# Experts' work between attention scores: smaller pieces, at least one in every round

## The chip, the cores and the metric

The kernel runs on one core of one Trainium2 chip. Its engines work side by side, each through its own queue in order: TensorE (PE; its weight loads are PEld in the profile), VectorE (DVE), ScalarE (ACT), GpSimd (POOL) and SyncE (SP, which here issues DMAs). They wait for each other through semaphores. The metric is the device time of one execution in microseconds, as the median of several runs. A profile is one further execution, taken by the hardware profiler; its span goes from the first to the last instruction.

## The reference

A block adds three things for 2048 tokens of 512 values: the input x, differential causal attention of the layer-normed x, and a mixture of experts of the layer-normed x. Cut to what matters here:

```
xn = layernorm(x)
# attention: 32 maps of 16 values, in pairs; 16 heads; causal
q, k = rotary(xn @ Wq), rotary(xn @ Wk);  v = xn @ Wv
a1 = softmax(mask(q1 @ k1.T * scale)) @ [v1, v2]
a2 = softmax(mask(q2 @ k2.T * scale)) @ [v1, v2]
f  = rfft(a1, tokens) - lambda * rfft(a2, tokens)
attn = irfft(f * gauss, tokens);  rms norm per head;  @ Wout
# experts: 8, the two best of each token, and a shared one of double width
y = sum over the two of w_e * (silu(xn @ w1[e]) * (xn @ w3[e])) @ w2[e]
shared = (silu(xn @ sw1) * (xn @ sw3)) @ sw2
out = x + attn + y + shared
```

## The kernel before

The kernel has a first part (layer norm, v, routing, rotated q and k, the shared expert for four of the 16 token tiles), the stage `middle`, and `ending` (the rest of the filter as products, the norm, the output projection, the sum). The change lies in `middle`. Of its two variants the one for scores of bounded size runs here, `middle(False)`. All five engines are under a manual schedule in it: each engine's instructions stand in the order in which the program issues them.

Attention goes through 32 chunks: for each of eight groups of two heads (`g`), four blocks of 512 queries (`qc`), the last block first. A chunk is a list of units. A unit is one tile of scores against 128 keys, for one head and both of its maps: two products on TensorE (L761) into one of two PSUM tiles, and one exponential on ScalarE (L774) into `pt`. Units on the diagonal, called masked, are narrower and are cut by GpSimd afterwards (L779). Chunks have 29, 21, 13 and 5 units, 544 in all. When both heads of a key block are there, their product with the values follows on TensorE (`values`, L801, into `ps_o`). VectorE adds the exponentials up (`added`, L818, or a copy L815 for the first). One round after a chunk's last values come its sums over keys (`sums`, L827) and, later in the same round, its `finish`: transposes of the output and of the sums (L839, L840), a reciprocal on VectorE (L842) and the normalised output `o_n` (L847). In the next round `put` (L856) adds the two halves into `vd` on GpSimd. When a group's four chunks are there, GpSimd does the first half of a Fourier transform over the 16 token tiles, in place (`folded`, L861 on, in seven steps). The last group's is on VectorE.

The main loop takes four units in each of 136 rounds. A round of the program before issues, in this order: a burst of two units; the values that the round before made ready, of one chunk; the sums of a closing chunk; a burst of the other two units; the remaining values; puts; additions; the `finish` of a closed chunk; experts' work until a budget is met, with the additions of the second two units between and behind its pieces; the additions of masked units; and up to two steps of folding.

Experts' work comes from a generator, `experts`. It yields after each piece the estimated time of that piece, and the loop asks for pieces as long as the time worked is behind the round's share of `work_all`. Its first 55 pieces are the shared expert's: `wh` (L231) and two halves of `wy` (L269) for each tile. The remaining ones are for 36 routed blocks of 128 tokens each. For block j these are:

- `up_first`: the product `xh` (L168), tanh on ScalarE (L175), a product on VectorE (L176)
- `up_third`: the product `xg` (L168), a product on VectorE (L182) that gives u; then the gather of the rows of block j + 2 on GpSimd (L585) and the fetch of up weights on SyncE
- `down` of block j - 1: the product `xy` (L201), scaled by ScalarE (L210) and stored; the fetch of down weights
- `turned_back` of block j: transposes of u on TensorE (L191) and two copies on VectorE (L193, L194)
- `transposed` of block j + 1: transposes of x on TensorE (L159) and a copy on ScalarE (L161)

The last three form one piece in the program before, after `xg`. All these tiles (`wh`, `wy`, `xh`, `xg`, `xy`, `ps_u`, `ps_x`) and also `ps_sum`, `ps_ot` and `ps_st` come from one PSUM pool of three banks, `fps`; a new tile takes the bank that was released first.

Of the kernel before, what the change touches and what calls it, by code (L numbers as in the profile page):

```python
# [19 lines left out]
P = 128  # L20
# [3 lines left out]
NT = T // P  # L24
# [3 lines left out]
TQ = QC // P  # L28
# [8 lines left out]
SCH = 6  # L37
TOP = 2
EARLY = 4
# [3 lines left out]
NR = NS - 3  # L43
# [19 lines left out]
def block_kernel(  # L63
# [17 lines left out]
    ys = dram.tile([NS * P, E], F32, name="ys")  # L81
# [16 lines left out]
    wcol = cpool.tile([P, NR], F32, name="wcol")  # L98
# [179 lines left out]
    with ExitStack() as pools:  # L278
# [231 lines left out]
        late = None  # L510
# [47 lines left out]
    def middle(general):  # L558


        with ExitStack() as pools:
# [29 lines left out]
            def experts():  # L591

                hidden = ExitStack()
                sp = hidden.enter_context(tc.tile_pool(name="shared", bufs=2))
                _, _, _, _, (_, _, stored), _ = expert(sp, fps, mp, by_scalar=True)
                _, _, _, chunks, result = shared_expert(sp, fps)
                for t0 in range(EARLY, NT - 1, TQ):
                    t1 = min(t0 + TQ, NT - 1)  # L600
                    last = t1 == NT - 1
                    cols = slice(t0 * P, t1 * P)
                    for n, us in enumerate(chunks(xnT[:, :, cols], u_last)):
                        if last and n == 0:
                            who_sb = mp.tile([P, E], F32, tag="x", name="who_sb")
                            who_sb = who_sb[:NR, : 2 * P].rearrange("n (p o) -> n p o", o=2)
                            nc.sync.dma_start(who_sb, who[: NR * P, :].rearrange("(n p) o -> n p o", p=P))
                        elif last and n == 3:
                            ps = bank([P, 2, NR], "ps_w")
                            for i in range(2):  # L610
                                nc.tensor.transpose(ps[:, i, :], who_sb[:, :, i], ident[:NR, :NR])
                            nc.vector.tensor_copy(tok, ps[:, 0, :])
                            nc.vector.tensor_copy(wcol, ps[:, 1, :])
                        elif last and n == 5:


                            xr = [rows_of(0), rows_of(1)]
                            es = [routed(0)]
                            fetch_up(es[0], 0, nc.sync)
                        yield 3.45 * (t1 - t0) / TQ  # L620
                    if last:
                        es.append(routed(1))
                        fetch_up(es[1], 1, nc.sync)
                    for t in range(t0, t1):
                        y = result(us, t - t0, range(NF))
                        yield 2.6
                        stored(result(us, t - t0, range(NF, SCH), y), ysh[t], 0.5)
                        yield 2.6
                hidden.close()
                rp = pools.enter_context(tc.tile_pool(name="routed", bufs=2))  # L630
                up_first, up_third, _, turned_back, (down, _, _), transposed = expert(rp, fps, mp, by_scalar=True)
                for i in range(2):
                    fetch_down(es[i], i, nc.sync)
                xT = transposed(xr.pop(0))
                yield 0.5
                for j in range(NR):
                    half = up_first(w_sb[j % 2][0], xT)
                    yield 2.4
                    u = up_third(w_sb[j % 2][0], xT, half)
                    if j + 2 < NR:  # L640
                        xr.append(rows_of(j + 2))

                    es.append(routed(j + 2) if j + 2 < NR else wex[NX + j + 2 - NR : NX + j + 3 - NR])
                    fetch_up(es[j + 2], j % 2, nc.sync)
                    yield 2.4
                    if j > 0:
                        down(*late)
                        fetch_down(es[j + 1], (j + 1) % 2, nc.sync)
                    uT = turned_back(u)
                    late = [(w_sb[j % 2][1], uT)], ys[j * P : (j + 1) * P, :], wcol[:, j : j + 1]  # L650
                    if j + 1 < NR:
                        xT = transposed(xr.pop(0))
                    if j == 1:
                        shared.append(True)
                    yield 3.7
                down(*late)
                yield 2.8

# [72 lines left out]
            class Chunk:  # L731
# [58 lines left out]
                def values(self, kb):  # L790

                    if self.done == 0:
                        self.o = vps.tile([P, QC], F32, tag="o", name="ps_o")
                    self.done += 1
                    first, self.ended = self.done == 1, self.done == (self.qc + 1) * TQ
                    for h in range(2):
                        v0 = 64 * self.g + 32 * h
                        pt, off = self.probs[h, kb]
                        for s in range(2):
                            r = 64 * h + 32 * s  # L800
                            nc.tensor.matmul(  # L801
                                self.o[r : r + 32, off:], vd[:, kb, v0 : v0 + 32], pt[:, s, :],
                                start=first, stop=self.ended, skip_group_check=True,
                            )
                    if self.ended:
                        self.o_sb = ap.tile([P, QC], F32, tag="o_sb", name="o_sb")
                        nc.scalar.copy(self.o_sb, self.o)
# [109 lines left out]
            for n, turn in enumerate(turns):  # L917
                chunk = Chunk(*turn)
                stream += [(n, chunk, unit) for unit in chunk.units()]
            work_all = (NT - 1 - EARLY) * ((2 * SCH - 1) * 3.45 / TQ + 5.2) + NR * 8.5 - 7.0  # L920
            ex = experts()
            for c in range(NQC):
                load_keys(0, c)
# [5 lines left out]
            def burst(units):  # L929
                nonlocal begun  # L930
                found = []
                for n, chunk, unit in units:
                    if n > begun:
                        begun = n
                        if n + 1 < len(turns):
                            load_queries(*turns[n + 1])

                        if chunk.g + 1 < NG:
                            load_keys(chunk.g + 1, (chunk.qc + 1) % NQC)
                    found += chunk.scores(unit)  # L940
                return found

            def values():

                chunk = todo[0][0] if todo else None
                while todo and todo[0][0] is chunk:
                    chunk.values(todo.pop(0)[1])
                return [chunk] if chunk is not None and chunk.ended else []

            def masked(entry):  # L950
                _, c, unit = entry
# [10 lines left out]
            for i in range(0, len(stream), 4):  # L962
                units = stream[i : i + 4]
                found = burst(units[:2])
                ended = values()
                for c in closing:
                    c.sums()
                    summed += 1
                found += burst(units[2:])
                while todo:  # L970
                    ended += values()
                todo += found
                for c in closed:
                    c.put(nc.gpsimd)
                    if c.qc == 0:
                        ready.append(c.g)
                closed, closing = closing, ended
                held, before = [], held
                added(before)
                added(u for u in units[:2] if not masked(u))  # L980
                later = [u for u in units[2:] if not masked(u)]
                for c in closed:
                    c.finish()
                while worked / work_all < (i + 4) / len(stream):
                    took = next(ex, None)
                    if took is None:
                        break
                    worked += took
                    added(later[:1])
                    later = later[1:]  # L990
                added(later)
                added(u for u in units if masked(u))
                for _ in range(0 if any(map(masked, units)) or not shared else 1 if len(ready) < 2 else 2):
                    if folding is None and ready:
                        folding = folded(ready.pop(0), nc.gpsimd)
                    if folding is not None and next(folding, 0) == 0:
                        folding = None
# [1 line left out]
                c.put(nc.gpsimd)  # L999
            ended = []  # L1000
            while todo:
                ended += values()
            for some in (closing, ended):
                for c in some:
                    c.sums()
# [369 lines left out]
```

## Time and profile before

| what | value |
|---|---|
| median of 3 runs | 1381.73 us (1381.63 to 1382.18) |
| the profiled execution's own time | 1382.72 us |
| its span | 1380.8 us |
| `middle`, by the first and the last product of its main part | 254.8 to 1262.6 us |
| units' products on TensorE (L761), busy | 209.9 us, 1280 matmuls |
| values (L801), busy | 270.7 us, 2560 matmuls |
| routed experts, xh, xg and xy, busy | 94.5, 93.2 and 103.5 us |
| additions on VectorE (L818), busy | 623.4 us, 576 instructions |
| exponentials on ScalarE (L774), busy | 528.1 us, 544 instructions |
| masks on GpSimd (L779), busy | 174.9 us, 256 instructions |

The rows with "busy" count the time in which at least one such instruction ran. Time of an engine before an instruction in which it did nothing is its idle time, and the profile names what ended it, written "<-" and the engine, tile and line that released it. The granted clock of TensorE is 1.00 or 0.50 in a window; its mean over the span is 0.987.

### The profile page before, as it was taken

What the parts mean: (1) busy time and instruction counts of PE and PEld (TensorE: products, weight loads), DVE (VectorE), ACT (ScalarE), POOL (GpSimd) and SP (SyncE); (2) the same over time, 40 slices, a digit from 0 to 9 for tenths busy, and PEclk for the clock granted to TensorE, in tenths of its full rate; (3) what the DMA queues carried; (4) which work ended last, traced back from release to release, by engine and by line L of the source; (5) the groups of instructions that cost most, each with busy time, mean ns of one, the idle gap of its engine ahead of it and who ended that gap; (6) DMA issues with size and microseconds to landing.
All of it is one profiled execution on the core that took longest, in us unless ns stands there. A gap on an engine that the chain in (4) does not pass through costs nothing.

```text
span 1380.8 us, 20566 instructions
## 1 busy us (share of the span) xinstructions
PE 1331.9 (96%) x7472; PEld 620.8 (45%) x7472; DVE 1005.4 (73%) x1337; ACT 692.7 (50%) x853; POOL 598.3 (43%) x673
## 2 busy tenths in 40 slices
PE   7999999899999999998899999999999999999998
PEld 3444444333443344444445444544454454445543
DVE  7059881368777776868677888867698779877785
ACT  2311110365656565665566566666667666662321
POOL 0002222012301232136975755757467537632874
PEclk9999999999999999999999999999999999999999
DMA  9406672200210121255455655656656565448996
GB/s 376 167 16 192 189 213 64 87 19 16 78 46 31 47 73 63 81 158 159 149 178 171 200 185 175 179 176 191 200 161 202 190 202 188 170 164 277 179 223 149
DMA packets 74689, 206.58 MB, mean 150 GB/s; under 512 B 12028, under 2 KB 12192, under 8 KB 69200
## 3 DMA queue, kind: packets, MB, share of 16 engines
q1 hardware_dynamic: 61840, 177.62, 39.4%
q0 software_dynamic: 11216, 23.31, 8.1%
q10 hardware_dynamic: 1520, 4.23, 0.9%
q8 instruction: 62, 1.02, 0.3%
q14 instruction: 51, 0.42, 0.1%
HBM read 161.26 MB, written 43.85 MB: 149 GB/s over the span
## 4 chain that ended last, share of the span: by engine, by line
PE 67%; DVE 5%; POOL 3%; DMA 3%; issue 2%; SPq 2%; ACT 2%; ACTq 0%; DVEq 0%; POOLq 0%
PE ps_o L801 17%; PE ps_s L761 12%; PE wh L231 8%; PE xy L201 6%; PE xh L168 6%; PE xg L168 6%; PE wy L269 4%; SPq L669 2%; PE ps_sum L827 2%; DVE sum L818 2%; ACT pt L774 1%; PE po L1196 1%; PE ps_ot L839 1%; PE ps_x L159 1%; DMA kS<-parts_k 1%
## 5 line engine op out<-in xcount | busy, mean ns | idle before, releaser
L818 DVE TENSOR_TENSOR sum<-sum,pt 128x1024 f32<-128x1024 f32 (+2 forms) x576 | 623.4, 1131 | 24.2 <-ACT pt L774 10.7
L774 ACT ACTIVATE pt<-ps_s 128x1024 f32<-128x1024 f32 x544 | 528.1, 1027 | 173.5 <-PE ps_s L761 128.1
L779 POOL TENSOR_SCALAR_AFFINE_SELECT pt<-pt 128x256 f32<-128x256 f32 x256 | 174.9, 708 | 340.5 <-ACT pt L774 277.5
L801 PE MATMUL ps_o<-pt,vd 128*32 128x512 f32 (+3 forms) x2560 | 270.7, 542 | 4.0 <-POOL pt L779 3.9
L761 PE MATMUL ps_s<-qS,kS 64*128 64x512 f32 (+3 forms) x1280 | 209.9, 411 | 14.7 <-ACT pt L774 12.9
L761 PEld LDWEIGHTS ps_s<-qS,kS 64*128 64x128 f32 x1280 | 97.8, 186 | 169.2 <-ACT pt L774 90.2
L231 PE MATMUL wh<-xnT,wu 128*128 128x512 f32 (+1 forms) x352 | 151.4, 578 | 0.0
L801 PEld LDWEIGHTS ps_o<-pt,vd 128*32 128x32 f32 x2560 | 67.2, 110 | 134.5 <-issue 115.5
L473 POOL DMA_INDIRECT who<-pairs,slot x32 | 34.3, 1073 | 202.0 <-DVE pairs L470 100.9
L520 PE MATMUL ps_x<-xnT,wqk_sb 128*128 128x512 f32 x256 | 110.5, 593 | 0.0
L201 PE MATMUL xy<-wd,uT 128*128 128x512 f32 (+1 forms) x216 | 103.5, 616 | 4.0 <-DVE rcp L842 4.0
L231 PEld LDWEIGHTS wh<-xnT,wu 128*128 128x128 f32 x352 | 64.9, 192 | 72.4 <-issue 57.3
L856 POOL TENSOR_TENSOR vd<-o_n 128x128 f32<-128x128 f32 x60 | 37.9, 653 | 137.2 <-DVE o_n L847 129.8
L168 PE MATMUL xh<-wu,xT 128*128 128x352 f32 x288 | 94.5, 471 | 0.7 <-ACT xT L161 0.7
L168 PE MATMUL xg<-wu,xT 128*128 128x352 f32 x288 | 93.2, 466 | 0.0
L520 PEld LDWEIGHTS ps_x<-xnT,wqk_sb 128*128 128x128 f32 x256 | 48.4, 190 | 60.6 <-issue 60.6
L269 PE MATMUL wy<-wd,ws 128*128 128x512 f32 x160 | 73.6, 601 | 0.0
L168 PEld LDWEIGHTS xh<-wu,xT 128*128 128x128 f32 x288 | 52.2, 191 | 33.6 <-issue 7.8
L168 PEld LDWEIGHTS xg<-wu,xT 128*128 128x128 f32 x288 | 52.6, 190 | 32.1 <-issue 4.3
L210 ACT ACTIVATE y_sb<-xy,wcol 128x512 f32<-128x512 f32 x36 | 24.8, 688 | 83.6 <-PE xy L201 83.6
L1052 POOL DMA_INDIRECT res<-ys,slot x32 | 56.6, 1769 | 21.0 <-DMA res<-ysh 10.4
L537 ACT CAST hi<-turned 128x1024 fp32r<-128x1024 f32 x16 | 16.7, 1045 | 93.8 <-DVE turned L535 83.1
(239 smaller groups left out, 1405.3 us busy)
## 6 DMA issues: line engine op xcount, KB each, us to landing
wu<-in_wex_dram SPq DMA_DIRECT2D x40, 1408.0 KB
wd<-in_wex_dram SPq DMA_DIRECT2D x39, 768.0 KB
kS<-parts_k SPq DMA_DIRECT2D x128, 128.0 KB
qS<-parts_q SPq DMA_DIRECT2D x256, 64.0 KB
ys<-y_sb SPq DMA_DIRECT2D x36, 256.0 KB
parts_q<-hi SPq DMA_DIRECT2D x32, 256.0 KB
parts_k<-hi SPq DMA_DIRECT2D x16, 256.0 KB
parts_k<-turned SPq DMA_DIRECT2D x16, 256.0 KB
```

The costliest lines, as they stand in the source:

```text
L168: nc.tensor.matmul(dst, xT[:, c, :], w[:, o : o + FI], start=(c == 0), stop=(c == NE - 1))
L201: nc.tensor.matmul(y, uT[:m, ic, :], w[:m, ic * E : (ic + 1) * E], start=(n == 0 and ic == 0), stop=(n == len(pairs) - 1 and ic == NF - 1),)
L231: nc.tensor.matmul(dst, w_sb[o // WUP][0][:, o % WUP : o % WUP + P], x[:, c, :], start=(c == 0), stop=(c == NE - 1))
L269: nc.tensor.matmul(y, us[i][:, t * P : (t + 1) * P], w_sb[i // NF][1][:, i % NF * E : (i % NF + 1) * E], start=(i == 0), stop=(i == SCH - 1),)
L520: nc.tensor.matmul(ps[:, i, :], wqk_sb[st, qk][:, i, c, :], xnT[:, c, cols], start=(c == 0), stop=(c == NE - 1),)
L761: nc.tensor.matmul(to, k, queries[2 * g + h, qc][r, off : off + w], start=True, stop=not general)
L774: nc.scalar.activation(pt[:, :, used], ps[:, :, used], AF.Exp, scale=SCALE)
L779: nc.gpsimd.affine_select(out=part, in_=part, pattern=[[0, 2], [1, P]], compare_op=ALU.is_ge, fill=0.0, base=0, channel_multiplier=-1,)
L801: nc.tensor.matmul(self.o[r : r + 32, off:], vd[:, kb, v0 : v0 + 32], pt[:, s, :], start=first, stop=self.ended, skip_group_check=True,)
L818: nc.vector.tensor_add(to, to, pt)
L856: eng.tensor_add(vd[:, self.qc * TQ : (self.qc + 1) * TQ, v0 : v0 + 32], self.o_n[:, :, h, 0, :], self.o_n[:, :, h, 1, :],)
L1052: nc.gpsimd.indirect_dma_start(out=came[k], out_offset=None, in_=ys, in_offset=bass.IndirectOffsetOnAxis(ap=slot[:, step - 2, order[k] : o ...
```

## The change

Four things change, all in `middle`.

1. In `experts`, a routed block's three pieces are cut elsewhere. The transposes of u of block j - 1 now stand at the head of block j's first piece, before `xh`; those of x of block j + 1 stand at the head of the third piece, before `xy` of block j - 1. The estimates become 2.9, 2.4 and 3.2 where they were 2.4, 2.4 and 3.7, and the budget `work_all` is 7.0 larger.
2. The loop asks for at least one piece in every round, also where the budget is already met.
3. Where the first values of a round are those of fewer than two key blocks, and no chunk is closing, one more piece is issued between the two bursts.
4. Two steps of folding in a round are taken only where none of the next round's units is masked.

```diff
@@ experts @@
-                xT = transposed(xr.pop(0))
-                yield 0.5
+                xT, late = transposed(xr.pop(0)), None
+                yield 0.6
                 for j in range(NR):
+                    if j > 0:
+                        late = [(w_sb[(j - 1) % 2][1], turned_back(u))], ys[(j - 1) * P : j * P, :], wcol[:, j - 1 : j]
                     half = up_first(w_sb[j % 2][0], xT)
-                    yield 2.4
+                    yield 2.9 if late else 2.4
                     u = up_third(w_sb[j % 2][0], xT, half)
...
                     yield 2.4
-                    if j > 0:
+                    if j + 1 < NR:
+                        xT = transposed(xr.pop(0))
+                    if late:
                         down(*late)
                         fetch_down(es[j + 1], (j + 1) % 2, nc.sync)
-                    uT = turned_back(u)
-                    late = [(w_sb[j % 2][1], uT)], ys[j * P : (j + 1) * P, :], wcol[:, j : j + 1]
-                    if j + 1 < NR:
-                        xT = transposed(xr.pop(0))
                     if j == 1:
                         shared.append(True)
-                    yield 3.7
+                    if late:
+                        yield 3.2
+                late = [(w_sb[j % 2][1], turned_back(u))], ys[j * P :][:P], wcol[:, j : j + 1]
+                yield 0.5
                 down(*late)
                 yield 2.8
@@ the loop @@
-            work_all = (NT - 1 - EARLY) * ((2 * SCH - 1) * 3.45 / TQ + 5.2) + NR * 8.5 - 7.0
+            work_all = (NT - 1 - EARLY) * ((2 * SCH - 1) * 3.45 / TQ + 5.2) + NR * 8.5
...
+            def work():
+                nonlocal worked
+                worked += next(ex, work_all)
...
                 found = burst(units[:2])
-                ended = values()
+                n, ended = values()
                 for c in closing:
                     c.sums()
                     summed += 1
+                if n < 2 and not closing:
+
+                    work()
                 found += burst(units[2:])
...
-                while worked / work_all < (i + 4) / len(stream):
-                    took = next(ex, None)
-                    if took is None:
-                        break
-                    worked += took
+                while True:
+                    work()
                     added(later[:1])
                     later = later[1:]
+                    if worked / work_all >= (i + 4) / len(stream):
+                        break
                 added(later)
                 added(u for u in units if masked(u))
-                for _ in range(0 if any(map(masked, units)) or not shared else 1 if len(ready) < 2 else 2):
+                if any(map(masked, units)) or not shared:
+                    steps = 0
+                else:
+                    steps = 1 if len(ready) < 2 or any(map(masked, stream[i + 4 : i + 8])) else 2
+                for _ in range(steps):
                     if folding is None and ready:
```

`values` now also returns how many key blocks it took.

More of the change, by code (lines that the diff above doesn't have):

```diff
@@ L943, in values @@
             def values():
-                chunk = todo[0][0] if todo else None
+                chunk, n = todo[0][0] if todo else None, len(todo)
                 while todo and todo[0][0] is chunk:
                     chunk.values(todo.pop(0)[1])
-                return [chunk] if chunk is not None and chunk.ended else []
+                return n - len(todo), [chunk] if chunk is not None and chunk.ended else []
+            def work():
+                nonlocal worked
+                worked += next(ex, work_all)
             def masked(entry):
@@ L968, in middle @@
                     summed += 1
+                if n < 2 and not closing:
+                    work()
                 found += burst(units[2:])
                 while todo:
-                    ended += values()
+                    ended += values()[1]
                 todo += found
@@ L1001, in middle @@
             while todo:
-                ended += values()
+                ended += values()[1]
             for some in (closing, ended):
```

## The prediction

> **What bounds the kernel now.** I read the page first, then the waits of TensorE between 255 and 1262 us (the stage that the change touches), its timeline around the longest of them, and the granted clock window by window.
>
> ```profile
> PE 1331.9 (96%) x7472; PEld 620.8 (45%) x7472; DVE 1005.4 (73%) x1337; ACT 692.7 (50%) x853; POOL 598.3 (43%) x673
> ...
> PE 67%; DVE 5%; POOL 3%; DMA 3%; issue 2%; SPq 2%; ACT 2%; ACTq 0%; DVEq 0%; POOLq 0%
> ```
>
> TensorE is busy for 96% of the span and carries the chain that ended last, and the change takes no matmul away. So a gain can only come from idle time of TensorE, and from its clock. In the stage, the idle time is this:
>
> ```profile
> PE ps_s L761 <- ACT pt L774: 12.9, 25, 2.2
> PE xy L201 <- DVE rcp L842: 4.0, 1, 4.0
> PE ps_o L801 <- POOL pt L779: 3.9, 2, 3.0
> PE ps_u L191 <- DVE rcp L842: 2.6, 1, 2.6
> PE ps_s L761 <- DVEq L1244: 1.7, 1, 1.7
> PE xh L168 <- ACT xT L161: 0.7, 1, 0.7
> PE ps_x L159 <- DVE o_n L847: 0.5, 1, 0.5
> PE ps_u L191 <- DVE xtanh L182: 0.3, 1, 0.3
> ```
>
> The columns are total us, times, longest. Together 26.6 us, half of them scores that wait for an exponential to free their PSUM tile. A wait costs more than its length, as the windows show (after the span: PE, PEld, DVE, ACT, POOL busy, then the clock):
>
> ```profile
> 901.30:904.70 3.40, 2.05 (x16) 0.76 (x20) 3.36 (x4) 2.91 (x4) 3.16 (x4) 0.99 0.12 39
> 904.70:908.10 3.40, 3.40 (x20) 0.89 (x12) 3.00 (x3) 0.86 (x1) 3.17 (x4) 0.50 0.80 185
> ...
> 976.30:979.80 3.50, 2.38 (x30) 1.03 (x30) 3.09 (x5) 3.40 (x4) 3.32 (x6) 1.00 0.94 344
> 979.80:983.20 3.40, 3.33 (x22) 1.53 (x19) 3.40 (x5) 2.43 (x3) 3.15 (x5) 1.00 0.47 110
> ```
>
> 1.35 us of idle in one window of 3.4 us is followed by a window at half clock, 1.1 us in another is not. A half window costs 1.7 us. The stage has eight: two at its start (256.1 to 262.9), two at 631.6, one each at 682.8, 775.0, 904.7 and 942.2.
>
> **The change, part by part.** I call a pass of the loop over four units a round and count from 0 to 135. Following both versions of the loop by hand gives the pieces in each round.
>
> *Waits for exponentials.* The 12.9 us are 2.23 in round 0, where nothing stands between the first two bursts; 0.34 in round 50; and the rest in the eight rounds with one pair of values between the bursts (8, 25, 42, 59, 76, 93, 110, 127; about 0.74 each, 1.71 in the one after the empty round 92) and behind the rounds without a piece (87, 97, 102: 1.34, 1.38, 0.66). The new loop puts a piece of at least 2.4 us into every one of these gaps, and two exponentials take 2 x 1.03 us. Only round 50 stays: -12.6. With them go the half windows at 904.7, 942.2 and the second at the start: -3 x 1.7 = -5.1.
>
> [...]
>
> *The order inside an expert's step.* Now u (three transposes, 0.33 us) stands ahead of the first product xh, and x (four, 0.44) ahead of the last, xy. A round or more lies between xg and u, and between x and xh: the waits of 0.7 (xT) and 0.3 (xtanh) go, -1.0.
>
> But three PSUM banks serve sums, ps_ot, ps_st and all experts' tiles. After a chunk's transposes (L839, L840) one bank is free; the next comes with the reciprocal L842, the third with o_n (L847), and both are behind the additions on VectorE:
>
> ```profile
> 760.88 0.27 PE L840 MATMUL ps_st<-cst,s_sb 128*128 128x128 f32 x1
> 760.99 2.53 PE L168 MATMUL xg<-wu,xT 128*128 128x352 f32 x8
> ...
> 768.13 2.74 PE L201 MATMUL xy<-wd,uT 128*128 128x512 f32 x6
> 773.43 0.55 PE L191 MATMUL ps_u<-cst,xtanh 128*128 128x128 f32 x3 [2.56 <-DVE rcp L842]
> ```
>
> ```profile
> 757.61 6.82 DVE L818 TENSOR_TENSOR sum<-sum,pt 128x768 f32<-128x768 f32 x6
> 764.34 1.29 DVE L815 COPY sum<-pt 128x1024 f32<-128x1024 f32 x2
> 765.55 0.26 DVE L842 RECIPROCAL rcp<-ps_st 128x16 f32<-128x16 f32 x1
> ```
>
> Round 68 needed one bank and did not wait, although the reciprocal came 4.65 us after ps_st; round 69 needed three and waited. Over all 32 chunks the reciprocal ends 0.30 us after ps_st in 16, 1.0 to 2.1 after in 13, and 6.33, 4.65 and 5.08 after in rounds 51, 68, 69. In the old order mostly one long product followed (cover 2.4 to 2.6 us). In the new one, 16 of the 21 turn-outs in the routed part begin with u or x, and the long product behind it needs the second bank after a cover of only 0.2 to 0.3 us. What I expect, lag minus cover, with the lag corrected for work moved before it:
> - 51: old lag 6.33, less 3.3 us more work in rounds 48 to 50: 2.9; 52: 0.5. 68: 4.65, less 1.6 (its round 67 has no tanh ahead of the additions, and 0.55 more work): 3.0; 69: 0.3.
> - 102: 1.5, 119: 0.7, 85: 0.2 (lags 1.36, 1.35, 2.13, moved by the rounds before); 48, where xh needs the third bank: 0.85.
> - 82, 94, 111, 128: VectorE takes its additions late behind a product of the same round, lags of 1.0 to 1.3: 3.3 together. The rest, at lag 0.3: 0.5 together.
>
> Sum 13.8, where the old waits (4.0 + 2.6 + 0.5) were 7.1: +6.7. Bounds: 5 if VectorE is on time in all but 51 and 68, so -2; 25 if it is late as below, so +18. I stay near the middle, because the lags of the trace are measured and only their shift is mine. These waits had three half windows (5.1), I expect two: -1.7.
>
> *Folding.* The step counts of all 136 rounds come out equal: wherever two steps ran, either no masked unit follows or only one head group was ready. This edit moves nothing. GpSimd still has an unbroken queue from 645 to 682 us and the masks of round 58 behind it; 0.6 us more work of TensorE before it: -0.6 of 3.9.
>
> *Switches.* In the chain a product behind scores takes 0.19 us longer than behind another product (xg 2.56 against 2.37, xy 2.77 against 2.58). Stretches of experts' work rise from 132 (four rounds had none) to 145 (one each, and nine between bursts): 13 x 0.19 = +2.5. If a switch from values costs nothing, +0.8.
>
> *The tail.* The old budget left xg, xy, u and xy to be done while the last two chunks close. From the end of the last scores (1245.4) to the first fold on VectorE (1261.6) took 16.3 us, all covered by TensorE. Now only u and xy (3.1) precede the values (2.3) and sums (0.9); additions end near 7.1 (8.2 before, with a tanh product and its wait ahead), then sums 1.0, copy 0.4, transposes 0.7, and 1.8 from reciprocal to fold: 11.0, so 5.2 less. But 2.56 + 2.56 + 2.77 = 7.9 us now lie before the last scores, and the last xy no longer hides beside the fold: +2.7. Bounds 0 and +6 (nothing of the closing shortened but 1.9).
>
> DMAs keep their number. The row gathers on GpSimd move with xg by a round or two, and land over 10 us before their use; the weight fetches on SyncE still have over 20 us to their product.
>
> **Sum**: -12.6 - 5.1 - 1.0 + 6.7 - 1.7 - 0.6 + 2.5 + 2.7 = -9.1 us on a span of 1380.8. The median of the runs is 1381.7 (the profiled execution 1382.7), so 1372.6.
>
> **Rivals.** (1) *The bank becomes the bound, slower.* If VectorE doesn't profit from the shifts in rounds 51 and 68/69 (6.1, 4.5, 1.5) and is one addition of 1.33 us later at half of the other 13 turn-outs (6.5 x 2.0), the waits are 25.1, and two more half windows follow: -9.1 + 11.3 + 3.4 = +5.6, 1387.3. It decides once the waits pass some 23 us. For it: an unmasked round asks VectorE for 4 x 1.33 + 0.52 = 5.8 us, and TensorE for 5.7 with one short piece. Against: in half the turn-outs VectorE was on time, since masked rounds leave it 2 to 4 us idle. (2) *No change.* The waits for exponentials leave, but the time comes back as waits for the bank, 7 to 10 us more than I allow, without the extra half windows: about 1381. (3) *Better.* The even pieces let VectorE be on time: waits of 5 us instead of 13.8, no half windows there (-3.4) and a neutral tail (-2.7): 1357.7 to 1364, by how much of it holds.
>
> **How the numbers follow.** Forecast 0.52 (its own range 1365 to 1379), rival 1 0.23, rival 2 0.15, rival 3 0.10. A measurement of this kernel can tell about 0.2%, 2.8 us. Faster: 0.52 + 0.10, 0.62; same 0.13 and slower 0.25, part of rival 2 falling on the slow side. The range 1363 to 1388 leaves out the best of rival 3 and the worst of rival 1.
>
> **What would show it.** Waits of ps_s for pt fall from 12.9 to under 1; xh L168 and xy L201 wait for the reciprocal in several places, 8 to 20 us together, the longest at the chunk ends of rounds 51 and 68; the mask wait of ps_o stays near 3.5; idle time of TensorE appears between the last scores and the fold. It is wrong if scores still wait, if the waits for the reciprocal pass 23 us, or if the fold starts as soon after the last scores as before.

## The result and the profile after

The changed kernel takes 1371.72 us (median of 6 runs, 1369.62 to 1375.6) where the kernel before takes 1381.95 in the same series (1381.14 to 1382.29): a ratio of 0.9916, 95% interval 0.9901 to 0.9931. The forecast was 1372.6. The profiled execution took 1372.31 us with a span of 1370.5, so 10.3 less of span than before.

The changed program is a few lines longer: L761 of before (scores) is L764 here, L842 (reciprocal) L845, L861 on (folding) L864 on. The experts' products keep their lines. First, from the page, the busy times and the chain that ended last:

```profile
PE 1325.6 (97%) x7472; PEld 614.9 (45%) x7472; DVE 1005.0 (73%) x1337; ACT 690.6 (50%) x853; POOL 565.9 (41%) x673
...
PE 68%; DVE 8%; issue 2%; ACT 1%; DMA 1%; POOL 1%; DVEq 0%; ACTq 0%
```

TensorE still sets the end; ScalarE's share of the chain fell from 2% to 1%, VectorE's rose from 5% to 8%. What TensorE waited for between 255 and 1262 us (total us, times, longest):

```profile
PE xh L168 <- DVE rcp L845: 7.9, 2, 4.6
PE ps_r L1082 <- issue: 5.2, 1, 5.2
PE xy L201 <- DVE rcp L845: 5.0, 3, 2.2
PE ps_s L764 <- DVEq L1258: 1.6, 1, 1.6
PE ps_o L804 <- POOL pt L782: 1.3, 1, 1.3
PE xh L168 <- ACT xT L161: 0.7, 1, 0.7
PE xy L201 <- DVE uT L193: 0.5, 1, 0.5
PE xy L201 <- DMA wd<-in_wex_dram: 0.5, 1, 0.5
```

The row of scores that wait for an exponential, 12.9 us before, is gone altogether. In its place stand five waits for a reciprocal, 13.0 us, where before such waits, with one of 0.5 us for o_n, came to 7.1. The 5.2 us of ps_r are new and stand behind the last score. The longest wait, at the end of the chunk in round 51, in the timeline:

```profile
624.61 0.66 PE L842 MATMUL ps_ot<-cst,o_sb 128*128 128x128 f32 x4
625.10 0.27 PE L843 MATMUL ps_st<-cst,s_sb 128*128 128x128 f32 x1
625.21 0.49 PE L191 MATMUL ps_u<-cst,xtanh 128*128 128x128 f32 x3
...
628.32 1.80 DVE L818 COPY sum<-pt 128x1024 f32<-128x1024 f32 x2
...
630.04 0.25 DVE L845 RECIPROCAL rcp<-ps_st 128x16 f32<-128x16 f32 x1
630.34 5.06 PE L168 MATMUL xh<-wu,xT 128*128 128x352 f32 x8 [4.64 <-DVE rcp L845]
```

The short transposes ps_u take the one free bank, xh needs the second and gets it only when the reciprocal has read ps_st, 4.91 us after ps_st ended. And xh then takes 5.06 us instead of some 2.6, because the clock has dropped (after the span: busy us of PE, PEld, DVE, ACT and POOL, then the clock):

```profile
628.80:632.20 3.40, 1.86 (x3) 1.18 (x4) 2.93 (x7) 0.00 (x0) 1.61 (x4) 0.50 0.90 239
632.20:635.60 3.40, 3.40 (x7) 2.02 (x6) 0.00 (x0) 0.16 (x1) 2.54 (x8) 0.50 0.19 70
```

By an estimate from xh, 5.06 us instead of some 2.6, half of the time in which TensorE was busy in these two windows is lost, (1.86 + 3.40) / 2 = 2.6 us, so this wait cost 4.64 + 2.6 = 7.3 us. A half window costs the whole 1.7 us only where TensorE does not wait in it. The wait of 3.30 at 759.6 is followed by two half windows as well; those of 2.18, 1.72 and 1.13 us by none.

The 10.3 us of span, set against the terms of the forecast:

| us | forecast | measured |
|---|---|---|
| idle time of TensorE, first to last score | -7.5 (-12.6 - 1.0 + 6.7 - 0.6) | -8.7 |
| half windows there (forecast: half of their length; measured: half of the time TensorE was busy in them) | -6.8 (-5.1 - 1.7) | -5.0 |
| products there | +10.4 (2.5 + 7.9) | +6.9 |
| last score to the end | -5.2 | -3.7 |
| before the first score | 0 | +0.2 |
| sum | -9.1 | -10.3 |

### The profile page after: what moved, and what is told of

It reads as the page before. It is cut to its first block, busy times and chain, and to the rows that moved or that the text cites. A ratio compares the mean times of both kernels' runs of the same rounds, so it can differ in the third digit from the quotient of the medians.

```text
span 1370.5 us, 20621 instructions
## 1 busy us (share of the span) xinstructions
PE 1325.6 (97%) x7472; PEld 614.9 (45%) x7472; DVE 1005.0 (73%) x1337; ACT 690.6 (50%) x853; POOL 565.9 (41%) x673
## 4 chain that ended last, share of the span: by engine, by line
PE 68%; DVE 8%; issue 2%; ACT 1%; DMA 1%; POOL 1%; DVEq 0%; ACTq 0%
PE ps_o L804 16%; PE ps_s L764 12%; PE wh L231 9%; PE xh L168 7%; PE xg L168 6%; PE xy L201 6%; PE wy L269 4%; DVE sum L821 3%; PE ps_sum L830 2%; PE po L1210 1%; DMA wd<-in_wex_dram 1%; PE ps_ot L842 1%; PE ps_u L191 1%; PE ps_z L1082 1%; PE ps_x L159 1%
## 5 line engine op out<-in xcount | busy, mean ns | idle before, releaser
L782 POOL TENSOR_SCALAR_AFFINE_SELECT pt<-pt 128x256 f32<-128x256 f32 x256 | 170.2, 689 | 331.5 <-ACT pt L777 276.0
L804 PE MATMUL ps_o<-pt,vd 128*32 128x512 f32 (+3 forms) x2560 | 266.0, 534 | 1.3 <-POOL pt L782 1.3
L764 PE MATMUL ps_s<-qS,kS 64*128 64x512 f32 (+3 forms) x1280 | 205.4, 407 | 2.0 <-DVEq L1258 1.6
L764 PEld LDWEIGHTS ps_s<-qS,kS 64*128 64x128 f32 x1280 | 97.2, 185 | 173.3 <-issue 95.1
L859 POOL TENSOR_TENSOR vd<-o_n 128x128 f32<-128x128 f32 x60 | 43.3, 742 | 172.4 <-DVE o_n L850 149.9
L201 PE MATMUL xy<-wd,uT 128*128 128x512 f32 (+1 forms) x216 | 99.8, 598 | 6.5 <-DVE rcp L845 5.0
L176 DVE SCALAR_TENSOR_TENSOR xtanh<-xtanh,xh 128x352 f32<-128x352 f32 x36 | 18.7, 520 | 67.2 <-ACT xtanh L175 67.2
L242 DVE SCALAR_TENSOR_TENSOR ws<-ws,wh 128x512 f32<-128x512 f32 (+4 forms) x26 | 16.8, 645 | 61.8 <-ACT ws L241 61.7
```

Source lines behind the costliest of these rows:

```text
L201: nc.tensor.matmul(y, uT[:m, ic, :], w[:m, ic * E : (ic + 1) * E], start=(n == 0 and ic == 0), stop=(n == len(pairs) - 1 and ic == NF - 1),)
L764: nc.tensor.matmul(to, k, queries[2 * g + h, qc][r, off : off + w], start=True, stop=not general)
L782: nc.gpsimd.affine_select(out=part, in_=part, pattern=[[0, 2], [1, P]], compare_op=ALU.is_ge, fill=0.0, base=0, channel_multiplier=-1,)
L804: nc.tensor.matmul(self.o[r : r + 32, off:], vd[:, kb, v0 : v0 + 32], pt[:, s, :], start=first, stop=self.ended, skip_group_check=True,)
L859: eng.tensor_add(vd[:, self.qc * TQ : (self.qc + 1) * TQ, v0 : v0 + 32], self.o_n[:, :, h, 0, :], self.o_n[:, :, h, 1, :],)
```

## Experiments

Each ratio is to the kernel before, run again in the same series: its median was 1381.95 us in the series of the changed kernel and 1382.0 to 1383.16 in the others. So kernels of different series are better compared by their ratios than by their medians; 0.001 is 1.4 us. "Idle" is the time between first and last score in which no matmul ran, "half" what the half windows there cost (half of the time in which TensorE was busy in them), "products" the rest of that stretch, "tail" the time from the last score to the end; all from the trace of each kernel's profiled execution, whose time is within the spread of its runs.

| kernel | median us | ratio, 95% interval | idle | half | products | tail |
|---|---|---|---|---|---|---|
| before | 1381.95 | | 25.1 | 12.3 | 953.2 | 135.4 |
| changed | 1371.72 | 0.9916 (0.9901 to 0.9931) | 16.4 | 7.2 | 960.0 | 131.7 |
| no piece between | 1382.80 | 1.0001 (0.9988 to 1.0013) | 26.2 | 7.5 | 961.5 | 132.5 |
| no floor | 1377.75 | 0.9958 (0.9942 to 0.9974) | 20.7 | 8.7 | 960.1 | 131.6 |
| old pieces, old budget | 1363.46 | 0.9863 (0.9847 to 0.9880) | 12.3 | 7.3 | 951.5 | 133.7 |
| long product first | 1362.17 | 0.9863 (0.9844 to 0.9882) | 11.7 | 1.7 | 960.0 | 132.5 |
| fold later | 1364.17 | 0.9864 (0.9848 to 0.9879) | 11.8 | 3.4 | 960.7 | 131.8 |
| old budget | 1370.65 | 0.9908 (0.9889 to 0.9927) | 19.6 | 7.8 | 955.2 | 130.8 |
| long first, fold later | 1358.66 | 0.9836 (0.9817 to 0.9855) | 6.3 | 3.4 | 959.0 | 132.1 |
| old pieces, fold later | 1359.38 | 0.9830 (0.9812 to 0.9847) | 9.4 | 7.3 | 951.3 | 133.3 |
| long first, fold later, wh later | 1358.31 | 0.9820 (0.9802 to 0.9838) | 6.9 | 3.1 | 959.4 | 131.8 |
| long first, fold later, old budget | 1363.29 | 0.9850 (0.9833 to 0.9868) | 15.0 | 8.8 | 954.1 | 130.9 |
| long first, fold later, wh later, old budget | 1364.91 | 0.9870 (0.9847 to 0.9894) | 13.9 | 8.8 | 954.0 | 135.8 |

### Which part of the change makes the gain

No piece between the bursts:

```diff
-                if n < 2 and not closing:
-
-                    work()
                 found += burst(units[2:])
```

> The changed kernel without the piece between the two bursts (1371.7 us with it). Theory: that piece is what took the waits for exponentials away, so they come back in round 0 (2.2 us) and in the eight rounds with one pair of values between the bursts (0.74 each): 8 us of waits of ps_s for pt, another half window or two, nine switches of 0.19 us less; 1378 to 1382 us. Rival: VectorE sets the pace, and the time only moves between waits: ps_s waits again, but the waits for the reciprocal fall by as much; 1370 to 1374 us.

It took 1382.8 us, a little above what was expected: without that piece the whole gain is gone. The waits of the scores are back, in TensorE's waits:

```profile
PE ps_s L764 <- ACT pt L777: 8.5, 17, 2.2
PE xh L168 <- DVE rcp L845: 7.9, 2, 4.5
PE xy L201 <- DVE rcp L845: 5.4, 4, 2.2
```

They cost more than they show: the scores' own products, counted to the start of the next product, took 2.7 us longer than in the changed kernel, some 0.16 for each of the 17 waits. Half of it lies in the score just ahead of a wait: nothing starts over its end, so it counts with all of its 0.49 us (mean of nine), where one that is followed at once counts with some 0.33.

No floor of one piece in a round (the loop asks for pieces only while behind the budget, as before):

```diff
-                while True:
+                while worked / work_all < (i + 4) / len(stream):
                     work()
                     added(later[:1])
                     later = later[1:]
-                    if worked / work_all >= (i + 4) / len(stream):
-                        break
```

> The changed kernel without the rule of at least one piece behind the second burst (the piece between bursts stays). All new pieces are smaller than a round's share, so the rule only acts in rounds 0, 8, 25, 42, 76, 110 and 127, where the piece between the bursts has run ahead of the share. Theory: there the next round's first burst follows with only one pair of values before it, so seven waits of ps_s for pt of 0.7 us and slower scores come back, 5 to 8 us: 1376 to 1380 us. Rival: the rule does nothing once pieces are small: 1370 to 1374 us.

1377.75 us, as the theory had it: eight waits for exponentials, 3.9 us, come back and 1.8 us of longer scores with them. The floor acts in seven rounds only (0, 8, 25, 42, 76, 110, 127), those that got a piece between the bursts and would have none behind the second; the trace has seven fewer stretches of experts' work (138, where the changed kernel has 145).

The loop's changes alone, with the pieces cut as before and the old budget:

```diff
+                if n < 2 and not closing:
+                    work()
                 found += burst(units[2:])
...
+                while True:
+                    work()
...
+                    if worked / work_all >= (i + 4) / len(stream):
+                        break
```

> The loop of the changed kernel (a piece in every round, one between the bursts) with the pieces and the budget of the kernel before. Theory: u and x at the head of a piece are what costs the second bank; with the old pieces mostly one long product follows a chunk's transposes, the waits for the reciprocal fall from 13.0 us to about 7 (rounds 51 and 69), waits for exponentials stay near zero, and four pieces are left to cover the closing of the last chunks, which returns 2 to 4 us: 1361 to 1367 us. Rival: the even, small pieces are what keeps VectorE on time; with the old ones the waits for the reciprocal stay at 13 us or grow: 1371 to 1378 us.

1363.46 us, some 7 us faster than the whole change by the ratios (0.9863 and 0.9916). So the loop is worth some 19 us, and cutting the pieces anew with the larger budget gave back about 7 of them. Its waits show why; the waits of before for the bank stay at 6.6 us:

```profile
PE xy L201 <- DVE rcp L842: 4.0, 1, 4.0
PE ps_u L191 <- DVE rcp L842: 2.6, 1, 2.6
...
PE ps_s L761 <- ACT pt L774: 0.3, 1, 0.3
```

### What makes the waits for the bank

Two things could be at fault: that a short piece of transposes takes the free bank just ahead of a long product, and that VectorE is late with the reciprocal. Each was changed alone. First the order, with the long product ahead of the transposes in the new pieces:

```diff
                 for j in range(NR):
+                    half = up_first(w_sb[j % 2][0], xT)
                     if j > 0:
                         late = ...
-                    half = up_first(w_sb[j % 2][0], xT)
...
-                    if j + 1 < NR:
-                        xT = transposed(xr.pop(0))
                     if late:
                         down(*late)
                         fetch_down(es[j + 1], (j + 1) % 2, nc.sync)
+                    if j + 1 < NR:
+                        xT = transposed(xr.pop(0))
```

> The changed kernel with the long product first in both pieces: xh before the transposes of u, xy before those of x. Theory: the free bank then goes to a product of 2.4 to 2.6 us, which covers the lag of the reciprocal; the waits of 1.1 to 2.2 us in rounds 82, 102 and 119 go, those of 51 and 68 fall from 4.6 and 3.3 us to about 2 and 1, and with them two to four half windows: 1358 to 1364 us. Rival: VectorE sets the pace there, and the wait moves to the next tile: 1369 to 1373 us, with u or x waiting for what xh and xy waited for.

1362.17 us. The cut itself was not at fault. No long product waits for a reciprocal any more:

```profile
PE ps_u L191 <- DVE rcp L845: 5.1, 2, 3.4
PE xh L168 <- ACT xT L161: 2.7, 3, 1.2
```

The reciprocal is no earlier (5.67 us after ps_st in round 51, 4.03 in 68; 4.91 and 3.57 in the changed kernel), but the 2.4 to 2.6 us of the long product lie over it. The price is in the second line: xT, made later, is waited for three times.

Then VectorE's lateness. In the rounds of the two longest waits, 51 and 68, GpSimd's folding additions run beside VectorE's, so the folding was left out in the five rounds that finish the chunks of block 1 with no mask (51, 68, 85, 102, 119):

```diff
-                if any(map(masked, units)) or not shared:
+                if any(map(masked, units)) or not shared or any(c.qc == 1 for c in closed):
                     steps = 0
```

> The changed kernel with no folding step in the five rounds (51, 68, 85, 102, 119) in which the chunk of the second query block is finished; the steps run one round later. Theory: the reciprocals of 51 and 68 are 4.9 and 3.6 us late because GpSimd's first folding additions hold up VectorE's; without them the lags fall to about 1.5 us, the two longest waits (4.6, 3.3 us) to about 1.3 each, and their four half windows go: 1360 to 1366 us. Rival: the lag is the masked additions themselves; lags and time stay, 1370 to 1374 us.

1364.17 us. The reciprocal now ends 0.98 us after ps_st in round 51 (4.91 in the changed kernel) and 1.06 in round 68 (3.57). In round 51, from the timeline of this kernel:

```profile
620.64 4.29 DVE L821 TENSOR_TENSOR sum<-sum,pt 128x768 f32<-128x768 f32 x6
...
625.05 0.27 PE L843 MATMUL ps_st<-cst,s_sb 128*128 128x128 f32 x1
...
626.06 0.25 DVE L845 RECIPROCAL rcp<-ps_st 128x16 f32<-128x16 f32 x1
...
626.36 2.63 PE L168 MATMUL xh<-wu,xT 128*128 128x352 f32 x8 [0.71 <-DVE rcp L845]
```

And what held VectorE up, one addition of the changed kernel between two of GpSimd's, in a narrow window of its timeline:

```profile
623.32 1.29 POOL L875 TENSOR_TENSOR xnT<-vd 128x512 f32<-128x512 f32 x1
623.44 2.69 DVE L821 TENSOR_TENSOR sum<-sum,pt 128x256 f32<-128x256 f32 x1
624.57 1.28 POOL L876 TENSOR_TENSOR xnT<-vd 128x512 f32<-128x512 f32 x1
```

The shortest addition of this size takes 0.42 us; this one took 2.69, began 0.12 us behind GpSimd's first and ended 0.28 us after its second. So VectorE's addition stalled beside GpSimd's, and the stall did not end with the first GpSimd addition at 624.61, it lasted through the second. What remains in this kernel is xy behind the reciprocal:

```profile
PE xy L201 <- DVE rcp L845: 7.2, 5, 2.4
```

Of these only 2.7 us are new (2.43 in round 94, 0.22 in 52). The rest stands in rounds 82, 102 and 119 (1.11, 1.72 and 1.71 us), where the changed kernel waited 1.13, 2.18 and 1.72. In this kernel GpSimd does no addition in the last 9 us before these three reciprocals, so folding is not what makes VectorE late in these three. With the old pieces the reciprocals of 102 and 119 came 1.36 and 1.34 us after ps_st, here 2.10 and 2.09: the new pieces lengthen them, and how was not taken apart.

Both together:

> The changed kernel with both edits that helped alone: the long product first (1362.2 us) and no folding in rounds 51, 68, 85, 102, 119 (1364.2 us). Theory: the first gives the lag of the reciprocal a cover, the second takes the lag away; both act on the same waits, so that they don't add up: what is left of the waits for the reciprocal after the first (5.4 us, one half window) goes, 1355 to 1359 us. Rival: they add up in full (7.5 + 9.5): 1354 us or less; or the folding that was pushed aside makes new waits elsewhere: 1361 us or more.

1358.66 us, and no wait for a reciprocal is left. What is late next is a weight load. In TensorE's waits, and in SyncE's queue:

```profile
PE xh L168 <- DMA wu<-in_wex_dram: 3.2, 3, 2.4
PE xh L168 <- ACT xT L161: 2.0, 2, 1.2
```

```profile
622.22 17.27 SPq L684 DMA_DIRECT2D qS<-parts_q  x8
639.53 2.38 SPq L672 DMA_DIRECT2D kS<-parts_k  x4
643.27 0.64 SPq L141 DMA_DIRECT2D wu<-in_wex_dram  x1
```

SyncE is held for 17.3 us at query loads, which wait mostly for earlier transfers (its waits there name kS with 8.3 us, wu with 3.1 and wd with 1.8), and the fetch of up weights stands behind them; at 659.1 xh waits 2.36 us, and one half window follows (659.2 to 662.6). In the changed kernel such waits for up weights don't show: the same fetch goes at 643.61 there, but its product only at 664.18.

The old pieces with the folding later:

> Old pieces and old budget in the new loop (1363.5 us), and no folding in rounds 51, 68, 85, 102, 119. Theory: the waits for the reciprocal of 4.0 and 3.1 us in rounds 51 and 69 and their three half windows (5.1 us) come from GpSimd's first folding additions and go, the wait of 4.1 us for masks stays or moves: 1350 to 1356 us. Rival: with the old pieces VectorE is late by itself: 1361 to 1364 us.

1359.38 us, above what the theory gave and below the rival. The reciprocal waits left as expected, but 4.7 us of waits for up weights came, and masks stay at 3.7. It is not to be told from the kernel above.

### What the work moved ahead of the last scores costs

The changed kernel with the old budget:

```diff
-            work_all = (NT - 1 - EARLY) * ((2 * SCH - 1) * 3.45 / TQ + 5.2) + NR * 8.5
+            work_all = (NT - 1 - EARLY) * ((2 * SCH - 1) * 3.45 / TQ + 5.2) + NR * 8.5 - 7.0
```

> The changed kernel with the old budget (7.0 less), so that the last three pieces (xy, u, xy, about 5.7 us of TensorE) are issued while the last chunks close. Theory: in the changed kernel 7.7 us of work moved ahead of the last scores and the closing became only 1.4 us shorter; with some of it back as cover the time falls by 3 to 5 us, less or more by up to 3 us for the other rounds in which pieces now fall: 1365 to 1370 us. Rival: the end is set by what follows the fold, and cover there is worth nothing: 1371 to 1374 us.

1370.65 us, just above the theory's range and below the rival's: no difference from the changed kernel that can be told. 4.9 us of products left the stretch ahead of the last score, and the tail did not grow (130.8 against 131.7): TensorE's idle time behind the last score falls from 10.2 to 6.4 us, so the work kept for the end is hidden there. But idle time between the scores grew by 3.2 us, since other pieces now fall into the rounds where a chunk ends.

With the reciprocal waits gone that should not matter, so it was tried again on the kernel of 1358.66 us, and with it the place of the wh products in the tail. In the changed kernel, timeline behind the last score (which ends at 1238.8):

```profile
1246.19 2.40 PE L231 MATMUL wh<-kept,wu 128*128 128x128 f32 x20
1248.43 0.27 PE L843 MATMUL ps_st<-cst,s_sb 128*128 128x128 f32 x1
...
1250.13 1.50 PE L231 MATMUL wh<-kept,wu 128*128 128x128 f32 x12
...
1253.60 0.69 DVE L875 TENSOR_TENSOR xnT<-vd 128x512 f32<-128x512 f32 x1
...
1256.99 3.58 PE L1082 MATMUL ps_r<-vd,conv 128*128 128x512 f32 x4 [5.24 <-issue]
```

The last fold starts 14.8 us after the last score, held up by 3.9 us of wh products in TensorE's order. The edit puts them behind the first products of the fold's result:

```diff
-            us = times(several((1, 3)), gated(several((0, 2))))
-            us = [us[:, :P], us[:, P:]]
             zr = pair("ps_r")
...
             diff = copied(at(2, fold, 6))
+            us = times(several((1, 3)), gated(several((0, 2))))
+            us = [us[:, :P], us[:, P:]]
```

> In the end of the core's work the gate's wh products stand in TensorE's order between the output transposes ps_ot and the sums' transposes ps_st of the last chunk, and the last fold waits for ps_st. In the changed kernel's profile they took 2.40 and 1.50 us there, and from the end of the last score to the first fold passed 14.8 us. This kernel is the one with the long products first and with no fold beside the waiting rounds (1358.66 us, 14.84 us in that stretch), with the wh products issued behind the differences' copy. Theory (the wh products stand in the fold's way, which is what the forecast's tail left out): the stretch falls to 10.5 to 12 us and the time to 1354 to 1357. Rival (what follows the fold needs wh just as early, so they only change places): the stretch falls, fold to end of the span grows by as much, and the time stays at 1358 to 1361.

1358.31 us: the rival holds. The fold starts 11.3 us after the last score, but in this kernel

```profile
1238.88 3.75 PE L1082 MATMUL ps_r<-vd,conv 128*128 128x512 f32 x4 [4.83 <-DVE vd L875]
...
1249.94 3.73 PE L231 MATMUL wh<-kept,wu 128*128 128x128 f32 x32
```

TensorE still waits 4.8 us for the fold, and the wh products take their 3.7 us behind it: fold to end grew from 117.3 to 120.5 us. They only changed places. Putting them into the wait itself, between ps_st and ps_r, was not tried.

The old budget on the kernel of 1358.66 us, and then both edits:

> The kernel with the long products first and no fold beside the waiting rounds (1358.66 us), with 7.0 us taken off the experts' budget as in the earlier run with the old budget, so that less of their work is moved ahead of the last scores. Theory (with the waits for the reciprocal gone nothing else is set by which round a piece falls into, so the 4 to 5 us of work kept for the end are a gain): idle time between first and last score stays within 1.5 us of 6.3, time 1353 to 1356. Rival (pieces that fall into other rounds meet other waits, as in the earlier run, where idle time grew by 3.2 us): idle time above 8.5 us, time 1357.5 to 1361.

> Both of the other two edits of this batch. Theory (they act in different stretches and add up): the sum of their two gains within 1.5 us, some 1350 to 1354 if both hold. Rival (work kept for the end and the wh products meet in the same stretch behind the last score and one takes the other's gain): no better than the better of the two, 1354 to 1359.

1363.29 and 1364.91 us, both above the range that the rival gave. The first is not clear of noise against the kernel without the old budget (0.9833 to 0.9868 and 0.9817 to 0.9855); the second is worse than the kernel with wh later (0.9847 to 0.9894 and 0.9802 to 0.9838). In the first the 4.8 us of products did leave the stretch (959.0 to 954.1), but idle time rose from 6.3 to 15.0 us. That trace is of the slowest of its runs, and the one that it is set against of the fastest, so the two differ more than the medians. The largest wait of the first of the two, in its timeline:

```profile
666.13 2.70 POOL L908 TENSOR_TENSOR vd<-vd 128x64 f32<-128x64 f32 x1
...
676.10 0.46 POOL L876 TENSOR_TENSOR xnT<-vd 128x128 f32<-128x128 f32 x1
676.50 5.07 POOL L782 TENSOR_SCALAR_AFFINE_SELECT pt<-pt 128x256 f32<-128x256 f32 x6
676.97 3.20 PE L804 MATMUL ps_o<-pt,vd 128*32 128x512 f32 x12 [5.38 <-POOL pt L782]
```

GpSimd's folding, which this kernel moved to other rounds, reached the masks late, and the values waited 5.38 us for the first of them. That this happens to the old budget and not to the new is probably a matter of which round each piece falls into; this was not shown, and why the folding ran later here was not taken apart further. With both edits the fold starts 13.2 us after the last score, as without the later wh, and from the fold to the end it takes 122.6 us instead of 117.6: there the wh products only add to the tail.

## Why the prediction was right, point by point

**Waits for exponentials, -12.6.** Right; all 12.9 went, round 50's too, and with them the three half windows at 904.7, 942.2 and the second at the start. Not foreseen: the scores around a wait also take longer. The products of the scores took 186.4 us instead of 190.2, 3.8 less, and the experiments without the piece or the floor give 2.7 us for 17 and 1.8 for 8 such waits.

**Order inside an expert's step, -1.0.** Wrong: the wait for xT stayed at 0.7 (round 48), that for xtanh went, and 0.5 for uT and 0.5 for down weights are new.

**The bank, +6.7.** Right in size (5.9: 13.0 against 7.1) and in mechanism, which the long-product-first run shows; wrong in its distribution. Round 51 took 4.64 (forecast 2.9), 68 3.30 (3.0), 102 2.18 (1.5), 119 1.72 (0.7); 82 1.13, where 82, 94, 111 and 128 together were given 3.3; 48, 52, 69 and 85 nothing, where they were given 1.85. So the sum came out near by luck: rounds 51, 68, 102 and 119 were 3.7 us too small, all others together 4.5 too large. The step that failed is the lag "corrected for work moved before it". In rounds 51 and 68 it fell by 1.4 and 1.1 us (6.33 to 4.91, 4.65 to 3.57), where 3.3 and 1.6 were taken off; in 102 and 119 it grew (1.36 to 2.57, 1.35 to 2.10). What keeps it long in 51 and 68 is GpSimd's folding, which the fold-later run shows (4.91 to 0.98 us, 3.57 to 1.06); that this is also why it fell less than foreseen is argued, not shown, and for 102 and 119 the cause stays open. The prediction saw the late additions and did not ask what made them late.

**Half windows.** -5.1 was right; "I expect two" behind waits for the bank was wrong, there are four (628.8 to 635.6 and 758.5 to 765.3). One that was to stay, at 682.8, went. The size was off too: the eight half windows before cost 12.3 us and not 8 x 1.7 = 13.6, since TensorE also waits in some of them.

**Folding and masks, -0.6.** The wait for a mask fell from 3.9 to 1.3, not to 3.3; why was not taken apart. That the folding edit moves no step was read off the rounds and not tested by itself.

**Switches, +2.5.** Right: the trace has 132 and 145 stretches of experts' work, as counted by hand. The kernel with old pieces and old budget also has 145, with nothing moved ahead, and its experts' products between first and last score took 2.4 us more than before. In the changed kernel they took some 3.5 us more than the 7.7 moved ahead; other products 0.5 less.

**The tail, +2.7.** Measured +4.0 (7.7 moved ahead, 3.7 won behind the last score). The step "11.0" from last score to fold left out the wh products between ps_ot and ps_st and a wait of 0.5 for uT: it took 14.8. But the run with wh later shows that even at 11.3 nothing is won, because TensorE has to do those products anyway. What the work moved ahead loses is cover: TensorE's idle time behind the last score went from 5.5 to 10.2 us.

**Rivals.** The bank as the bound (waits over 23 us) did not come; it had 13.0. The better case, with VectorE on time, is what the fold-later and long-product-first runs reach (1364.2 and 1362.2 us), and both together, at 1358.7 us, come close to the best of its range. "No change", in which the time comes back as waits for the bank, did not come either: these grew by 5.9 us, less than the 6.7 allowed.

So the mechanism held, and the time was met within 1 us partly by luck, because errors of both signs cancelled: by the table of the terms, idle time came out 1.2 and products 3.5 us better than forecast, half windows 1.8, the tail 1.5 and the start 0.2 worse.

## What to carry to other kernels

When work is cut into smaller pieces to fill waits, look at what each piece needs at its start: a short piece that takes the last free buffer moves the wait to the long piece behind it, and putting the long one first gave some 7 us here (0.9916 to 0.9863 of the kernel before). When an engine is late only in some places, ask which other engine runs beside it in just those; here that answered for the two longest waits and not for the others. Work moved ahead of the last barrier is only a gain if nothing covered it behind; here it was covered.

## What was not expected of the hardware

- GpSimd is held up as well as VectorE. One addition of 128x64 (L908, at 666.13 above) took 2.70 us, while VectorE did two additions (666.30 to 668.65), and 0.32 in the kernel with long products first and the folding later; one of 128x128 (L889) 0.46 in the former and 5.07 in the latter, while VectorE did four (645.75 to 650.37).
- Half-clock windows start at multiples of some 3.41 us from each other, wherever the waits lie (256.8, 628.8, 758.5, 1256.9). The wait of 2.18 us at 1005 fell on two such windows, with 1.36 us idle in one and 0.82 in the next, and cost no clock; before, 1.35 us idle ahead of 904.7 did. So near 1.35 us other things decide, which these runs don't show. Counted on each trace's own grid between 250 and 1262 us, in all thirteen traces, a window at full clock in which TensorE was idle for 1.87 us or more was followed by one at half clock each time (32 of 32), and one with less than 1.06 us idle never; in between it was 16 of 50, the shortest with 1.06 us (ahead of 942.2 in the kernel before). So the two rows of the prediction, 1.35 and 1.1 us, don't mark a limit between them.
